# Attention: 4 of a unit's 16 transfers of turned weights issued by ScalarE, the other 12 by SyncE

## The chip, the cores and the metric

The kernel runs on one NeuronCore of a Trainium2 chip. The core has a matrix engine (TensorE, PE in the profile; its weight loads are shown apart as PEld), a vector engine (VectorE, DVE), an activation engine (ScalarE, ACT), a general engine (GpSimd, POOL) and an engine that mostly issues DMA transfers (SyncE, SP). Each engine works through its own list of instructions in order; semaphores tie the lists together. Data moves between HBM and the on-chip memory (SBUF, 128 partitions), and from one place of SBUF to another, by 16 DMA engines, which transfers issued by SyncE and ScalarE reach by a queue each. Matmuls write into PSUM, eight banks of 128 x 512 floats.

The metric is device time in microseconds, as the median of several runs. The profiler records one further execution instruction by instruction.

## The reference

The model is a "macaron" block in float32: half a feed-forward block, causal attention, half a feed-forward block again, on 16 sequences of 512 tokens of width 256. Only the attention bears on the change:

```python
x = x + 0.5 * ffn(layernorm(x))
x = x + attn(layernorm(x))          # the change is in here
x = x + 0.5 * ffn(layernorm(x))

def attn(x, Wq, bq, Wkv, bkv, Wo, bo):            # 16 heads, 64 wide
    q = x @ Wq + bq
    k, v = split(x @ Wkv + bkv)
    q, k = rope(q), rope(k)
    scores = einsum('bhqd,bhkd->bhqk', q, k) / sqrt(64)
    scores = where(causal, scores, -inf)
    probs = softmax(scores)
    out = einsum('bhqk,bhkd->bhqd', probs, v)
    return out.reshape(b, s, 1024) @ Wo + bo
```

## The kernel before

The program has three stages: the first feed-forward block, attention (from about 450 to 1930 us of the span) and the second feed-forward block. The change touches attention alone.

Attention is cut into 64 units: 16 sequences times four groups of four heads. A unit's weights, that is its softmax probabilities, are four tiles of 128 query rows (tile i has (i+1) x 128 keys, the causal part) for each of four heads. The loop over u near the end of `attention` is a pipeline written out by hand: in one turn of it the kernel makes queries and keys of unit u+3, scores and probabilities of unit u+2, turns the probabilities of unit u+1, and multiplies the turned ones of unit u by v and by the output weights. The order of the calls in that loop is the order of each engine's list; no scheduler moves them.

The steps by name and line:

- `scores` (L1047, L1054, TensorE) writes the products of queries and keys into PSUM banks p_as, tile 3 first, then 2, and in a later place tiles 1 and 0.
- `exps` (L1073, L1077): for each head and tile VectorE adds the mask, takes the row's extreme (amn) and moves the scores from PSUM to SBUF (pr), which empties the bank; ScalarE then makes the exponentials and their row sums (ars).
- `scaled` (L1082, L1085): VectorE inverts the sums, GpSimd multiplies pr by them.
- `turn`, `turn_most`, `turn_corner`, `turn_tile` (L1100, VectorE): the probabilities must stand with the keys on the partitions before they can be multiplied by v. VectorE can transpose squares of 32 x 32 within a group of 32 partitions; it writes the turned squares into the tile sq.
- `move` (L1127, SyncE): the squares of sq still have to change groups of partitions. 16 transfers do that: for each group k of 32 partitions of the result prT and each group q of sq, 32 rows of 5,120 bytes, 160 KB. All 16 move 2.6 MB, from SBUF to SBUF. They are issued when the last turn of the unit, `turn_tile(0)`, is done.
- `sums` (L1158, TensorE, p_av) multiplies prT by v; ScalarE copies the result to aoT (L1169).
- `leave` (L1176, TensorE, p_ay; L1182, VectorE): multiplies aoT by the output weights and adds to x; after a sequence's last group SyncE stores x (L1184).
- `values` (L1010 TensorE, L1013 ScalarE) makes v of the next unit.
- `Trip` (L961 VectorE, L964 and L970 SyncE) turns the normalized input of a coming sequence by way of HBM: one transfer out (away) and sixteen back (ahT), eight in each of two units, every fourth unit.

sq and prT have one buffer each, shared by all units. So the first turn of the next unit, `turn_most(0)`, can begin only when all 16 transfers have read sq, and the first transfer only when `sums` of the unit before has read prT. SyncE issues in one list, in this order: the 16 transfers of a unit, then, in some units, the write of away, two stores of x and eight reads of ahT.

The lines of the loop around the change:

```python
                if new:
                    new.scores((3,))
                    new.scores((2,))
                    new.exps((3,), slice(0, 1))
                if old and 0 <= u < nu - 2:
                    old.turn_tile(0)
                    old.move()
                if new:
                    new.exps((3,), slice(1, 2))
```

The transfers go out between the first and the second head's exponentials of tile 3 on ScalarE's side; ScalarE has its exponentials of heads 1 to 3 of tile 3 and of all heads of tile 2 still to do then.

Of the kernel before, what the change touches and what calls it, by code (L numbers as in the profile page):

```python
# [9 lines left out]
F32 = mybir.dt.float32  # L10
# [5 lines left out]
P = 128  # L16
# [18 lines left out]
HG = 4  # L35
NHG = AH // HG
SQ = 32
NSQ = P // SQ
# [9 lines left out]
def macaron_kernel(ctx: ExitStack, tc: tile.TileContext, a: dict, out: bass.AP):  # L48
    nc = tc.nc
# [835 lines left out]
    def attention(qp, wq, wk, wv, wo, cos, sin, row):  # L885


        ap = None
# [22 lines left out]
        nu = len(units)  # L911
        hTs, hs, qs, ks, vs, oTs, prTs, stds, trips = {}, {}, {}, {}, {}, {}, {}, {}, {}
# [11 lines left out]
        def scales(g, std):  # L924

            n = PB * NT
            rstds[g] = small.tile([P, n], F32, tag=f"rstd{g}", name=f"rstd{g}", bufs=1)
            nc.vector.reciprocal(rstds[g], std)
            pair_shift(g)

        def enter(b):

            hs[b] = [qp.tile([P, 2, D], F32, tag=f"rope{2 + k}", name=f"h{b}_{k}") for k in range(2)]
            for t in range(NT):
                i = (b % PB) * NT + t
                nc.scalar.activation(hs[b][t // 2][:, t % 2, :], xs[b][:, t, :], AF.Identity,
                                     bias=shifts[b // PB][:, i:i + 1], scale=rstds[b // PB][:, i:i + 1])
# [5 lines left out]
        def width(b):  # L943
            hTs[b] = qp.tile([P, NC, S], F32, tag="hT", name=f"ahT{b}", bufs=2)
            for c in range(NC):
                pt = ps(f"p_ahT{b}_{c}")
                for t in range(NT):
                    nc.tensor.transpose(pt[:, t * P:(t + 1) * P], hs[b][t // 2][:, t % 2, c * P:(c + 1) * P], ident)
                nc.scalar.copy(hTs[b][:, c, :], pt)  # L949
# [52 lines left out]
        def values(u, t0):  # L1002
            b, hg = units[u]
            if t0 == 0:
                pool, tag, bufs = (ap, "v", 1) if u + 1 < nu else (qp, "hT", 2)
                vs[u] = pool.tile([P, NT, HG * DQ], F32, tag=tag, name=f"v{b}_{hg}", bufs=bufs)
            pv = ps(f"p_v{b}_{hg}_{t0}")
            for t in range(2):
                for k in range(NC):
                    nc.tensor.matmul(pv[:, t * 256:(t + 1) * 256], hTs[b][:, k, (t0 + t) * P:(t0 + t + 1) * P],  # L1010
                                     wv[:, k, hg * HG * DQ:(hg + 1) * HG * DQ],
                                     start=(k == 0), stop=(k == NC - 1))
            nc.scalar.copy(vs[u][:, t0:t0 + 2, :].rearrange("p t d -> p (t d)"), pv)  # L1013
# [4 lines left out]
        blocks = NT * (NT + 1) // 2  # L1018
# [3 lines left out]
        class Weights:  # L1022
# [96 lines left out]
            def move(self):  # L1119

                prT = prTs[self.u] = ap.tile([P, NSQ, HG, blocks * SQ], F32, tag="prT", name=f"prT{self.nm}")
                for n in range(NSQ):
                    for k in range(NSQ):
                        q = (k + n) % NSQ
                        nc.sync.dma_start(prT[k * SQ:(k + 1) * SQ, q, :, :], self.sq[q * SQ:(q + 1) * SQ, k, :, :])  # L1127

            def turn_at_once(self, tag, vector):

# [59 lines left out]
        def queries_keys(u):  # L1190

            if u >= nu:
                return []
            q = qs[u] = Rotated(u, "q", wq, R_BQ)
            k = ks[u] = Rotated(u, "k", wk, R_BK)
            return [lambda: q.half(0), lambda: (q.half(1), q.add()), lambda: k.half(0), lambda: (k.half(1), k.add())]
# [4 lines left out]
        ap = yield [lambda: width(0)] + queries_keys(0)  # L1201
        ws = {}
        seen = 2 * NHG
        with tc.tile_pool(name="awayh", bufs=2, space=bass.MemoryType.DRAM) as away, \
                tc.manual_schedule(engines={mybir.EngineType.DVE, mybir.EngineType.Activation,
                                            mybir.EngineType.Pool, mybir.EngineType.SP}):
            for u in range(-2, nu):
                new = ws[u + 2] = Weights(u + 2) if u + 2 < nu else None
                qk = queries_keys(u + 3)
                old = ws.get(u + 1)  # L1210

                fresh = units[u + 5][0] if NHG < u + 5 < nu and units[u + 5][1] == 0 else 1 if u + 3 == NHG else None

                stats = [divmod(at, NHG) for at in range(seen, min(u + 15, NB * NHG))]
                seen = max(seen, u + 15)
                left = [divmod(u - NHG - 1, NHG)] if u >= NHG + 1 else []
                if u + 2 == nu:
                    old.scaled((1, 0))
                    values(u + 1, 0)
                    values(u + 1, 2)  # L1220
                if u >= 0:
                    sums(u, 0)
                    sums(u, 1)
                if fresh:
                    enter(fresh)
                if u + 4 in trips:
                    trips[u + 4].land((0, 1))
                if u + 3 in trips:
                    trips[u + 3].land((2, 3))
                if old and u + 2 == nu:  # L1230
                    old.turn_at_once("sq", range(0, 10, 2))
                elif u == -1:
                    values(0, 0)
                    values(0, 2)
                    old.turn_at_once("prT", range(2, 10, 3))
                elif old:
                    old.scaled((1, 0), slice(0, HG // 2))
                    old.turn_most(1)
                    old.turn_most(2)
                    old.scaled((1, 0), slice(HG // 2, HG))  # L1240
                    old.turn_most(3)
                    old.turn_corner()
                    old.turn_tile(1)
# [9 lines that stand above are left out]
                gone = [leave(u, 0)] if u >= 0 else []  # L1253
                if fresh == 1:
                    width(1)
                if u >= 0:
                    gone.append(leave(u, 2))
                if new:
                    new.exps((3,), slice(2, HG))
                    new.exps((2,), halfway=lambda: new.scaled((3,)))  # L1260
                if u == -2:
                    new.scaled((2,))
                    new.scores((1, 0))
                    new.exps((1, 0))
                    new.scaled((1, 0))
                if u + 6 in stds:
                    scales((u + 6) // (PB * NHG), stds.pop(u + 6))
                if fresh and fresh > 1:
                    trips[u + 5] = Trip(fresh)

                if u == nu - NHG + 1:
                    for g in range(NB // PB - 1):
                        pair_rstd(g)
                if u == nu - 1:
                    for g in range(PB):
                        entered[g] = xs[g]
                        for t in range(NT):
                            i = (g % PB) * NT + t
                            nc.vector.tensor_scalar(xs[g][:, t, :], xs[g][:, t, :], mvs[g // PB][:, i, 0:1],
                                                    rstds[g // PB][:, i:i + 1], ALU.subtract, ALU.mult)  # L1280
                for one in gone:
                    one()
                if new and u > -2:
                    new.scaled((2,))
                for one in stats + left:
                    token_stats(*one)
                for one in qk:
                    one()
                if fresh:
                    with_bias(fresh)  # L1290
                if NHG < u + 7 < nu and (u + 7) % (PB * NHG) == 0:
                    stds[u + 7] = spread((u + 7) // (PB * NHG))
                if 0 <= u < nu - 2:
                    values(u + 1, 0)
                    values(u + 1, 2)
                if new and u > -2:
                    new.scores((1, 0))
                    if u + 3 < nu:
                        new.turn_most(0)
                    new.exps((1, 0))  # L1300
            token_stats(NB - 2, NT - 1)
# [55 lines left out]
```

## Time and profile before

| what | us |
|---|---|
| runs | 2311.49, 2314.21, 2315.38 |
| median of the runs | 2314.21 |
| the profiled execution, its time | 2317.09 |
| its span, first to last instruction | 2315.4 |
| attention, 460 to 1890 us of the span: TensorE busy | 1417.9 of 1430 |
| the same: VectorE, ScalarE, GpSimd busy | 1269.4, 780.2, 845.1 |
| the same: mean share of the 16 DMA engines | 0.55 |
| granted TensorE clock, mean | 0.995 of full speed |
| transfers prT<-sq | 992 (62 units x 16), 160 KB each |

How to read it: a row of the profile names the line, the engine, the operation and the tiles, output before input. Behind the bar stand the busy time and the mean duration of one, then the idle time of the engine before such instructions and what ended it. "SPq" and "ACTq" are DMA issues, which occupy an engine's list but are not counted as busy time. A timeline row gives start, duration, engine, line, operation and, in brackets, the idle time before it with its releaser. Matmuls overlap in the hardware, so a busy TensorE row says that it was not starved, not that it ran at its peak.

Two of the 64 units turn their probabilities on TensorE (`turn_at_once`), so 62 have transfers.

### The profile page before, as it was taken

How to read it: one execution, taken by the hardware profiler on the slowest of the kernel's cores; microseconds unless marked ns; L12 is line 12 of the kernel's file. 1: busy time of each engine (PE TensorE's matmuls, PEld its weight loads, DVE VectorE, ACT ScalarE, POOL GpSimd, SP SyncE). 2: the span in 40 equal slices, each digit the busy share in tenths (PEclk: the TensorE clock that was granted, in tenths of full speed). 3: DMA queues.
4: the chain of work that ended last, by engine and by line, in shares of the span. 5: the costliest groups of instructions: out<-in, count | busy, mean ns of one | idle time of the engine just before them, and what ended most of it. 6: DMA issues, size and time to landing. Idle time of an engine off the chain costs nothing. (4 is left out here: it accounts for less than half of the span.)

```text
span 2315.4 us, 52884 instructions
## 1 busy us (share of the span) xinstructions
PE 2254.7 (97%) x19544; PEld 1488.2 (64%) x19544; DVE 1761.6 (76%) x4678; ACT 1158.1 (50%) x3296; POOL 1068.6 (46%) x1695
## 2 busy tenths in 40 slices
PE   7999999999999999999999999999999999998999
PEld 4764488566666666666666666666666666764588
DVE  5742298788889898989898988989888875432387
ACT  5753243455555555556464545555555555532233
POOL 2210054565566556565656565656556542210043
PEclk9999999999999999999999999999999999999999
DMA  6839851055556465554655554646455543739734
GB/s 209 261 112 403 339 140 55 7 131 121 130 127 147 110 148 130 122 140 111 146 129 129 128 140 111 158 97 160 120 132 130 124 115 112 237 138 404 305 116 140
DMA packets 221929, 359.52 MB, mean 155 GB/s; under 512 B 99876, under 2 KB 159848, under 8 KB 213480
## 3 DMA queue, kind: packets, MB, share of 16 engines
q1 hardware_dynamic: 220812, 355.34, 55.3%
q8 instruction: 155, 2.54, 0.5%
q14 instruction: 102, 0.84, 0.1%
q10 hardware_dynamic: 860, 0.81, 0.1%
HBM read 156.29 MB, written 37.22 MB: 84 GB/s over the span
## 5 line engine op out<-in xcount | busy, mean ns | idle before, releaser
L1085 POOL TENSOR_SCALAR pr<-pr,ars 128x512 f32<-128x512 f32 (+3 forms) x1024 | 524.1, 532 | 575.0 <-DVE ars L1082 573.8
L1077 ACT ACTIVATE pr<-pr,amn 128x512 f32<-128x512 f32 (+3 forms) x1024 | 561.8, 550 | 219.6 <-DVE amn L1073 215.2
L1100 DVE STREAM_TRANSPOSE sq<-pr 128x768 f32<-128x768 f32 x434 | 384.5, 918 | 130.1 <-DMA prT<-sq 106.7
L1073 DVE CUSTOM_DVE_ANT_0 pr<-p_as,causal 128x512 f32<-128x512 f32 (+2 forms) x768 | 308.6, 457 | 7.0 <-PE p_as L1054 5.8
L1054 PE MATMUL p_as<-k,q 32*64 32x448 f32 (+3 forms) x8192 | 307.3, 414 | 0.0
L1158 PE MATMUL p_av<-prT,v 128*64 128x512 f32 (+3 forms) x2048 | 291.5, 437 | 10.1 <-ACT pr L1077 2.0
L1013 ACT COPY v<-p_v 128x512 f32<-128x512 f32 x128 | 74.6, 585 | 451.3 <-PE p_v L1010 451.3
L1158 PEld LDWEIGHTS p_av<-prT,v 128*64 128x64 f32 x2048 | 161.1, 137 | 139.6 <-issue 92.7
L1176 PE MATMUL p_ay<-wo,aoT 128*128 128x256 f32 x1024 | 238.6, 386 | 4.1 <-DVE amn L1073 3.0
L1010 PE MATMUL p_v<-wv,ahT 128*128 128x256 f32 x1024 | 231.6, 379 | 0.7 <-DVE x L1182 0.7
L988 PE MATMUL p_q<-ahT,wq 128*128 128x512 f32 x512 | 230.6, 593 | 0.2 <-ACT ahT L949 0.2
L1054 PEld LDWEIGHTS p_as<-k,q 32*64 32x64 f32 x8192 | 201.8, 131 | 45.0 <-issue 26.2
L988 PE MATMUL p_k<-ahT,wk 128*128 128x512 f32 x512 | 230.3, 592 | 0.0
L1176 PEld LDWEIGHTS p_ay<-wo,aoT 128*128 128x128 f32 x1024 | 189.2, 190 | 62.2 <-DVE amn L1073 37.0
L1010 PEld LDWEIGHTS p_v<-wv,ahT 128*128 128x128 f32 x1024 | 194.5, 190 | 53.8 <-issue 23.7
L1077 ACT ACTIVATION_READ_ACCUMULATOR pr<-pr,amn 128x1 f32 x1024 | 192.0, 187 | 0.0
L988 PEld LDWEIGHTS p_k<-ahT,wk 128*128 128x128 f32 x512 | 97.3, 190 | 122.0 <-issue 106.9
L988 PEld LDWEIGHTS p_q<-ahT,wq 128*128 128x128 f32 x512 | 97.0, 190 | 95.7 <-issue 78.6
L1073 DVE CUSTOM_DVE_ANT_1 pr<-p_as,causal 128x384 f32<-128x384 f32 x256 | 130.2, 546 | 0.0
L1169 ACT ACTIVATE aoT<-p_av,bcol 128x128 f32<-128x128 f32 (+1 forms) x384 | 117.1, 391 | 9.9 <-PE p_av L1158 9.9
L584 PE MATMUL p_ds<-hT,qk 128*128 128x512 f32 x256 | 118.8, 609 | 2.1 <-ACT hT L159 2.1
L811 PE MATMUL p_cy<-vw,catT 128*128 128x256 f32 x512 | 120.8, 379 | 0.0
(179 smaller groups left out, 3358.0 us busy)
## 6 DMA issues: line engine op xcount, KB each, us to landing
prT<-sq SPq DMA_DIRECT2D x992, 160.0 KB
w<-in_e_W_dram SPq DMA_DIRECT2D x64, 1024.0 KB
w<-in_e_Wg_dram SPq DMA_DIRECT2D x32, 1024.0 KB
out_dram<-x SPq DMA_DIRECT2D x64, 256.0 KB
awaya<-sqa SPq DMA_DIRECT2D x25, 512.0 KB
atT<-awaya SPq DMA_DIRECT2D x100, 128.0 KB
xl<-in_attn_x_dram SPq DMA_DIRECT2D x16, 512.0 KB
xl<-out_dram SPq DMA_DIRECT2D x16, 512.0 KB
```

The lines of the kernel that those rows point to most:

```text
L584: nc.tensor.matmul(psc, qk[:, k, c * P:(c + 1) * P], hT[:, k, :], start=(k == 0), stop=(k == NC - 1))
L811: nc.tensor.matmul(py[:, t * D:(t + 1) * D], atT[:, c, t * P:(t + 1) * P], vws[b][:, c, :], start=(c == 0), stop=(c == NC - 1))
L988: nc.tensor.matmul(pq, self.w[:, k, at:at + P], hTs[self.b][:, k, :], start=(k == 0), stop=(k == NC - 1))
L1010: nc.tensor.matmul(pv[:, t * 256:(t + 1) * 256], hTs[b][:, k, (t0 + t) * P:(t0 + t + 1) * P], wv[:, k, hg * HG * DQ:(hg + 1) * HG * DQ], s ...
L1054: nc.tensor.matmul(banks[j][half * H:(half + 1) * H, at:at + wh], q[n][rows, q0:q0 + H], k[n][rows, :wh], start=(n == 0), stop=(n == 1))
L1073: nc.vector.tensor_tensor_reduce(out=by_block(self.at(i, j)), in0=by_block(banks[j][:, at:at + w]), in1=mask(i), scale=-1.0 / math.sqrt(DQ ...
L1077: nc.scalar.activation(self.at(i, j), self.at(i, j), AF.Exp, bias=self.mn[:, i, j:j + 1], scale=-1.0, accum_out=self.rs[:, i, j:j + 1])
L1085: nc.gpsimd.tensor_scalar(self.at(i, j), self.at(i, j), self.rs[:, i, j:j + 1], 1.0, ALU.mult, ALU.mult)
L1100: nc.vector.transpose(view(self.sq, j * blocks * SQ + dst[0] * SQ, [(blocks * SQ, nh)] + [(s * SQ, n) for s, (_, n) in zip(dst[1:], of)] + ...
L1158: nc.tensor.matmul(po[j * DQ:(j + 1) * DQ, :].rearrange("d (a f) -> d a f", a=NSQ)[:, :, t * SQ:], vs[u][:, t, head * DQ:(head + 1) * DQ], ...
L1169: nc.scalar.activation(dst[:, odd, to], src[:, odd, of], AF.Identity, bias=bcol[:, r:r + 1])
L1176: nc.tensor.matmul(py[:, t * D:(t + 1) * D], oTs[u][:, pair, (t0 + t) * P:(t0 + t + 1) * P], wo[:, hg * (HG // 2) + pair, :], start=(pair ...
```

## The change

`move` now issues twelve of the sixteen transfers on SyncE: those of the first three rounds n. The four of the last round (n = 3) become a function of their own, `move_rest`, in another order of k, and go to ScalarE's queue. `move_rest` is called after the exponentials of tile 2, so ScalarE issues them when it has done those. What each transfer copies is as before.

```diff
-                prT = prTs[self.u] = ap.tile([P, NSQ, HG, blocks * SQ], F32, tag="prT", name=f"prT{self.nm}")
-                for n in range(NSQ):
-                    for k in range(NSQ):
-                        q = (k + n) % NSQ
-                        nc.sync.dma_start(prT[k * SQ:(k + 1) * SQ, q, :, :], self.sq[q * SQ:(q + 1) * SQ, k, :, :])
+                prTs[self.u] = ap.tile([P, NSQ, HG, blocks * SQ], F32, tag="prT", name=f"prT{self.nm}")
+                self.send(nc.sync, [(k, (k + n) % NSQ) for n in range(NSQ - 1) for k in range(NSQ)])
+
+            def move_rest(self):
+
+                self.send(nc.scalar, [(k, (k + NSQ - 1) % NSQ) for k in (2, 3, 0, 1)])
+
+            def send(self, queue, ways):
+                for k, q in ways:
+                    queue.dma_start(prTs[self.u][k * SQ:(k + 1) * SQ, q, :, :],
+                                    self.sq[q * SQ:(q + 1) * SQ, k, :, :])
...
                 if new:
                     new.exps((3,), slice(2, HG))
                     new.exps((2,), halfway=lambda: new.scaled((3,)))
+                if old and 0 <= u < nu - 2:
+                    old.move_rest()
                 if u == -2:
```

## Prediction

> **What bounds the kernel now.** I read the busy shares and costliest groups of the page first, then the attention stage (460 to 1890 us, where all the moved transfers are issued) in the table by windows, then one unit engine by engine in the timelines.
>
> ```profile
> PE 2254.7 (97%) x19544; PEld 1488.2 (64%) x19544; DVE 1761.6 (76%) x4678; ACT 1158.1 (50%) x3296; POOL 1068.6 (46%) x1695
> ...
> L1100 DVE STREAM_TRANSPOSE sq<-pr 128x768 f32<-128x768 f32 x434 | 384.5, 918 | 130.1 <-DMA prT<-sq 106.7
> ...
> L1176 PEld LDWEIGHTS p_ay<-wo,aoT 128*128 128x128 f32 x1024 | 189.2, 190 | 62.2 <-DVE amn L1073 37.0
> ```
>
> TensorE is nearly always busy, but two waits show beside it: VectorE waits 106.7 us for the transfers prT<-sq, and TensorE's weight loads for p_ay wait 37.0 us for VectorE. They are one loop. Here is a unit whose transfers begin at t0 = 1047.09, SyncE, VectorE and TensorE in turn:
>
> ```profile
> 1047.09 10.05 SPq L1127 DMA_DIRECT2D prT<-sq  x16
> ...
> 1060.97 0.98 DVE L1100 STREAM_TRANSPOSE sq<-pr 128x768 f32<-128x768 f32 x1 [2.10 <-DMA prT<-sq]
> 1062.04 0.42 DVE L1073 CUSTOM_DVE_ANT_0 pr<-p_as,causal 128x256 f32<-128x256 f32 x1
> ...
> 1060.43 0.22 PE L1047 MATMUL p_as<-blank 32*64 32x64 bf16 x4
> ...
> 1069.72 1.99 PE L1176 MATMUL p_ay<-wo,aoT 128*128 128x256 f32 x8
> ```
>
> The 16 transfers are issued in 10.05 us; the turn of head 0 (turn_most(0), which overwrites sq) can start only when all have landed, at t0+13.88. After it come the row maxima of tiles 1 and 0, and 7.68 us after the first of them (1062.04) p_ay starts, as soon as VectorE has emptied a bank of tile 3 (1069.00 + 0.65). So the loop is: landing, turn, maxima, turns, bank, p_ay, next t0.
>
> I listed these starts for all 61 units from the timelines. Between successive p_ay the 60 intervals sum to 1405.3 us; the usual one is 23.26, so 9.7 us in all lie above it. Usually the maxima start 1.61 us after TensorE's p_as for tiles 1 and 0 (1060.43 to 1062.04): the matmuls set the pace, and a landing some 0.17 us later would cost nothing (the turn needs about 0.9 us before the maxima, so it may start up to t0+14.04; the median of the 33 units of 60 that meet this is t0+13.88). The other 27 of 60 turns start later. In the 25 later than t0+14.1 the interval grows nearly one for one, 8.8 us in all. One such unit, t0 = 578.66:
>
> ```profile
> 593.23 0.98 DVE L1100 STREAM_TRANSPOSE sq<-pr 128x768 f32<-128x768 f32 x1 [2.78 <-DMA prT<-sq]
> ...
> 601.78 1.56 PE L1176 MATMUL p_ay<-wo,aoT 128*128 128x256 f32 x6 [0.21 <-DVE amn L1073]
> ```
>
> The turn starts at t0+14.57, p_ay at t0+23.12 instead of t0+22.63. What counts is therefore one number, the landing of the last of 16. Shifting all 61 turn starts and summing what lies above 14.04 gives the price: earlier by 0.2 us -4.7 us, by 0.5 us -8.7, never more than -9.8; later by 0.13 us +4.6, by 0.2 us +7.6, by 0.4 us +18.8. There is no more to gain than 9.8 us, as TensorE's own work sets 23.26.
>
> What sets the landing is seen in the table by windows of the first unit (time, PE, PEld, DVE, ACT, POOL, clock, share of the 16 DMA engines, GB/s):
>
> ```profile
> 1047.10:1048.20 1.10, 1.10 (x7) 0.97 (x6) 1.10 (x5) 0.76 (x3) 0.00 (x0) 1.00 0.00 0
> 1048.20:1050.00 1.80, 1.80 (x10) 1.59 (x9) 1.69 (x9) 1.80 (x7) 0.00 (x0) 1.00 0.94 205
> 1050.00:1052.00 2.00, 2.00 (x6) 0.95 (x5) 2.00 (x7) 2.00 (x7) 1.81 (x3) 1.00 0.95 276
> 1052.00:1054.00 2.00, 2.00 (x6) 0.88 (x5) 1.85 (x7) 1.95 (x5) 2.00 (x5) 1.00 0.97 223
> 1054.00:1056.00 2.00, 2.00 (x6) 0.83 (x5) 2.00 (x4) 1.39 (x2) 1.54 (x3) 1.00 1.02 225
> 1056.00:1058.00 2.00, 2.00 (x9) 1.37 (x8) 2.00 (x4) 0.00 (x0) 2.00 (x2) 1.00 1.05 228
> 1058.00:1060.00 2.00, 2.00 (x11) 1.77 (x10) 0.87 (x2) 0.58 (x1) 1.88 (x3) 1.00 0.82 177
> 1060.00:1061.00 1.00, 1.00 (x31) 0.67 (x37) 0.03 (x1) 0.46 (x1) 0.69 (x1) 1.00 0.02 5
> ```
>
> Nothing moves for 1.1 us after the first issue; then the DMA engines are full, at about 223 GB/s, until just before 1060. 16 transfers of 163,840 bytes at 223 GB/s are 11.8 us, 0.735 each, while SyncE issues one each 10.05/16 = 0.63 us. The engines, not the issuing queue, are the limit, and a queue of about a microsecond of work stands before them from the middle on. 1.1 + 11.8 leaves 1.0 of the 13.88 us for the start-up and for the last completion to reach VectorE.
>
> **The change, part by part.** Call SyncE's transfers S0 to S11 and ScalarE's A0 to A3.
>
> *Taken off SyncE*: four issues of 0.63 us, 2.5 us a unit. Since the engines are full, the issues shorten nothing by themselves: 0.
>
> *Put on ScalarE*: four issues behind its exponentials of tile 2. Its six issues at the start of the kernel took 0.24 to 0.59 us, so 1.0 to 2.4 us a unit, plus 239 more semaphore instructions in the build, about four a unit, at 17 to 28 ns (SyncE's shortest and median at L1127): 0.1. The exponentials end at t0+5.18 in nearly every unit and ScalarE's next work, the copy of v, follows 6.59 us after (1005.4 to 1012.00 in the unit of t0 = 1000.23). In every eighth unit two table loads, a square root and an exponential (3.1 us) stand between, and 3.4 us of idle time remain. Hidden: 0. Without that cover the copy of v would be late, then av behind it on TensorE, 1.0 to 2.5 us a unit.
>
> *The wait that is added*, not seen in the diff. The build gives DMAs eight completion semaphores in turn, and each DMA waits until the one before it on its semaphore has landed. In 61 of 62 units the turns are taken in the order S0 S1 S2 S3 A0 S4 A1 S5 A2 S6 A3 S7 S8 S9 S10 S11. So S8 waits for A0's landing and S10 for A1's; A2 and A3 wait for S0 and S2, long landed. S8 is no longer issued at t0+5.0: A0 goes out at about t0+5.3, its data can move from t0+6.4, and S7 is still in the engines until 1.1 + 0.4 + 8 x 0.735 = t0+7.4 (0.4 us for the start-up). A0, sharing them with S6 and S7, is done by t0+8.1 and landed by about t0+8.6; S8 follows 3.6 us later than now, with data from t0+9.7. By then the engines have A1 to A3 to do, until 1.5 + 12 x 0.735 = t0+10.3. So they do not run dry, by 0.6 us. S9 to S11 come 0.63 us apart and are served 0.735 apart; the sixteenth ends at 1.5 + 11.8 = t0+13.3 and lands at t0+13.9, as now: 0. Bounds: earlier by 0.5 us if the queues together move more than one (-8.7), later by 0.3 us if the engines run dry for that long (+12.9). I take 0, because the share of 0.94 to 1.05 leaves no room in the one direction and the 0.6 us is room in the other.
>
> *Behind S11 on SyncE* stand the write of turned x (L964), two stores of y (L1184) and eight reads back (L970), now about a microsecond later (S11's issue ends at t0+11.2, not 10.05). In the unit of t0 = 1000.23 the reads began at 1016.06, took 4.85 us, and the next transfers of turned weights went out at 1023.83: 2.9 us free, so 0; with it gone, the next t0 is late one for one.
>
> *Order elsewhere*: VectorE's and GpSimd's instructions and waits are the same in both builds; TensorE's are too, but for a wait or two.
>
> *The late units.* 20 of the 992 issues on SyncE took 0.92 to 1.70 us instead of 0.59, mostly 96 instructions apart, and 16 KB instruction transfers of 0.9 to 1.3 us lie among them; one DMA engine then ends later than the others. SyncE has 248 instructions fewer (1804 instead of 2052), ScalarE 487 more: two to three such fetches fewer here, five more there, each worth 8.8/25 = 0.35 us when it meets the transfers, about half the time on ScalarE. Sum 0, bounds -1 and +2.
>
> **A rule and the rows.** A1 writes partitions 96 to 127 while S8 writes 0 to 31, so they might use different paths. No transfer from two queues at once is in this trace; the windows stay at 223 to 228 GB/s although neighbours on one queue already write different halves. The Trainium skill, "DMA: Bandwidth & Descriptors", Rules for kernel authors, speaks against the change: two transfers to disjoint partition halves serialize, since both use the same 16 engines, from one queue or two. The skill's "SBUF — State Buffer", "Can I just issue two DMAs to hit both halves?", gives 6% for such a pair; on the four transfers that would be an estimated 0.18 us a unit, some -4 us by my price list, where the rows say 0.
>
> **Sum.** 0 against the profiled execution: span 2315.4 us, its time 2317.1 with 1.7 us around it. The median of the runs, 2314.2, lies 2.9 us below that, so I forecast 2314 us.
>
> **Rivals.** *Faster*: two queues keep the DMA engines better filled; the last landing comes 0.5 us earlier, the late units vanish, 2314.2 - 8.7 = 2305.5 us. For it: 27 late turns are there to be saved, and A0 to A3 are out before S8. Against: the full share; A0 and A1 write the same half as S6 and S7, A3 the same as S8.
> *Slower*: the wait of S8. If A0 lands after about t0+9.2, S8 brings its data after the engines have run dry, and each further tenth delays the last landing by a tenth. With A0 at t0+9.6 the landing is 0.4 us late: 2314.2 + 18.8 = 2333 us; 0.2 us gives 2322. For it: A0 depends on ScalarE's issue, nowhere measured beside work, and passes through a queue that SyncE's backlog shares. Against: it needs 0.6 us more than the rows give.
> *ScalarE held up*: its four issues outlast 6.59 us; it would take 1.6 us each against at most 0.59 seen. Under 2 in 100, counted as slower.
>
> **How the numbers follow.** No change 0.46, faster 0.27, slower 0.27. About 0.2%, 4.6 us, is what a measurement can tell from no change; by the price list that is a landing between 0.2 us earlier and 0.13 us later, a narrow gate for a forecast of this kind, which is why no change does not get more. Its own range is 2310 to 2318; for 8 in 10 it reaches over the faster case to 2305 and into the slower one to 2326.
>
> **What would show it.** Right: SyncE's transfers split 8 and 4, with a gap of about 3.5 us waiting for ScalarE's; VectorE's wait for prT<-sq still near 2 us; p_ay intervals of 23.26. Wrong on the faster side: more than 240 GB/s over 2 us while both queues are at work, and turn starts before t0+13.5. Wrong on the slower side: a DMA share clearly below 0.9 near t0+9 to t0+11, turns after t0+14.1 in most units and more than 37 us of weight loads waiting for VectorE.

## The result and the profile after

The changed kernel takes 2324.0 us (median of 5 runs, 2322.2 to 2328.0); the kernel before, beside it, 2314.2 (2311.5 to 2316.0). The ratio is 1.0043, 95% interval 1.0028 to 1.0058: slower by 9.8 us, where no change was forecast. The profiled execution took 2327.98 us, with a span of 2326.3.

From the page of the changed kernel, busy times of the engines, the first two DMA queues (packets, MB, share of the 16 engines' span) and two of the costliest groups:

```profile
PE 2259.2 (97%) x19544; PEld 1482.4 (64%) x19544; DVE 1759.7 (76%) x4678; ACT 1158.7 (50%) x3296; POOL 1072.3 (46%) x1695
...
q1 hardware_dynamic: 208908, 314.69, 47.7%
q10 hardware_dynamic: 12764, 41.45, 8.0%
...
L1100 DVE STREAM_TRANSPOSE sq<-pr 128x768 f32<-128x768 f32 x434 | 385.1, 918 | 148.6 <-DMA prT<-sq 102.5
...
L1182 PEld LDWEIGHTS p_ay<-wo,aoT 128*128 128x128 f32 x1024 | 189.1, 190 | 69.9 <-DVE amn L1073 45.8
```

ScalarE's queue (q10) now carries its quarter. VectorE idles 148.6 us before its turns instead of 130.1; the row names the releaser of most of it, the transfers prT<-sq, whose own figure even falls (106.7 to 102.5); the view of waits puts 37.9 us instead of 23.4 down to ahT<-away. TensorE's weight loads for p_ay wait 45.8 us for VectorE instead of 37.0. So the same loop is longer. The 60 intervals between successive p_ay sum to 1418.5 us instead of 1405.3 (+13.2). With t0 as the moment at which a unit's first transfer goes out, the start of turn_most(0) has its median at t0+14.41 instead of t0+14.01, and 47 of 60 turns start after t0+14.1 instead of 26. Here is the unit of t0 = 1170.09, which has this median, in the timelines of SyncE, ScalarE, VectorE and TensorE:

```profile
1170.09 4.31 SPq L1132 DMA_DIRECT2D prT<-sq  x7
...
1175.13 0.51 SPq L1132 DMA_DIRECT2D prT<-sq  x1
...
1178.13 2.74 SPq L1132 DMA_DIRECT2D prT<-sq  x4
...
1174.34 0.52 ACTq L1132 DMA_DIRECT2D prT<-sq  x1
1174.48 0.19 ACT L1077 ACTIVATION_READ_ACCUMULATOR pr<-pr,amn 128x1 f32 x1
1174.58 0.60 ACT L1077 ACTIVATE pr<-pr,amn 128x384 f32<-128x384 f32 x1
1174.89 0.61 ACTq L1132 DMA_DIRECT2D prT<-sq  x1
1175.08 0.19 ACT L1077 ACTIVATION_READ_ACCUMULATOR pr<-pr,amn 128x1 f32 x1
1175.54 1.33 ACTq L1132 DMA_DIRECT2D prT<-sq  x2
...
1184.51 0.98 DVE L1100 STREAM_TRANSPOSE sq<-pr 128x768 f32<-128x768 f32 x1 [2.64 <-DMA prT<-sq]
...
1193.07 2.21 PE L1182 MATMUL p_ay<-wo,aoT 128*128 128x256 f32 x9 [0.22 <-DVE amn L1073]
```

Three things are to be seen. SyncE's list has gaps: S0 to S6 go out as before, S7 at t0+5.04, S8 only at t0+8.04. A0 goes out at t0+4.25, while ScalarE still has its last exponential of tile 2 to do (1174.58 to 1175.18): the issues run ahead of the engine's own work. So it is not right that ScalarE issues them when it has done the exponentials, as the section on the change says. And the turn starts at t0+14.42, so that p_ay waits.

The landings of the single transfers, taken from the semaphore events in the trace (medians over 60 units), say where S7 and S8 stood: S3 lands at t0+5.05 and S7 goes out at 5.07; A0 lands at 8.05 and S8 goes out at 8.06; A1 lands at 9.21 and S10 goes out at 9.46 (within a unit 0.02 to 0.7 us behind A1, 0.1 in the median). The last of the 16 lands at t0+14.12 instead of t0+13.84.

### The profile page after: what moved, and what is told of

Same layout as the page of the kernel before. It is cut to its first block, busy times and chain, and to the rows that moved or that the text cites. A ratio compares the mean times of both kernels' runs of the same rounds, so it can differ in the third digit from the quotient of the medians.

```text
span 2326.3 us, 53123 instructions
## 1 busy us (share of the span) xinstructions
PE 2259.2 (97%) x19544; PEld 1482.4 (64%) x19544; DVE 1759.7 (76%) x4678; ACT 1158.7 (50%) x3296; POOL 1072.3 (46%) x1695
## 5 line engine op out<-in xcount | busy, mean ns | idle before, releaser
L1100 DVE STREAM_TRANSPOSE sq<-pr 128x768 f32<-128x768 f32 x434 | 385.1, 918 | 148.6 <-DMA prT<-sq 102.5
L1013 ACT COPY v<-p_v 128x512 f32<-128x512 f32 x128 | 74.8, 586 | 437.5 <-PE p_v L1010 430.9
L1182 PEld LDWEIGHTS p_ay<-wo,aoT 128*128 128x128 f32 x1024 | 189.1, 190 | 69.9 <-DVE amn L1073 45.8
L1054 PEld LDWEIGHTS p_as<-k,q 32*64 32x64 f32 x8192 | 193.5, 131 | 48.2 <-issue 30.6
```

The lines of the kernel that those rows point to most:

```text
L1054: nc.tensor.matmul(banks[j][half * H:(half + 1) * H, at:at + wh], q[n][rows, q0:q0 + H], k[n][rows, :wh], start=(n == 0), stop=(n == 1))
L1100: nc.vector.transpose(view(self.sq, j * blocks * SQ + dst[0] * SQ, [(blocks * SQ, nh)] + [(s * SQ, n) for s, (_, n) in zip(dst[1:], of)] + ...
L1182: nc.tensor.matmul(py[:, t * D:(t + 1) * D], oTs[u][:, pair, (t0 + t) * P:(t0 + t + 1) * P], wo[:, hg * (HG // 2) + pair, :], start=(pair ...
```

## The experiments

A transfer writes 32 partitions of prT (group k) and reads 32 partitions of sq (group q). Groups 0 and 1 lie in the lower half of the partitions (L), 2 and 3 in the upper (U). The packets of 5,120 bytes take 351 ns on average instead of 341. In the later part of a unit of the kernel before, they take 380 to 400 ns where neighbouring transfers write one half, and the time dips to 310 to 330 where the half changes. Read transfer by transfer in the order of issue, the written halves are LLUU LLUU LLUU LLUU before, and LLUU LLUU UULL LLUU in the change: ScalarE's order k = 2, 3, 0, 1 puts S6, S7, A0 and A1 into U, and A2, A3, S8 and S9 into L. So there are three theories. **A**, order of halves: a transfer is slower behind one of the same half, and the change puts four in a row. **B**, waits: S7, S8 and S10 go out late and the DMA engines run short. **C**, two queues: serving two queues costs by itself.

The first four runs set them against each other. The last landing is in each case the median over the units, counted from t0.

**e1, the split kept, ScalarE's order 0, 1, 2, 3** (written halves as before, in the order of the code):

```diff
-                self.send(nc.scalar, [(k, (k + NSQ - 1) % NSQ) for k in (2, 3, 0, 1)])
+                self.send(nc.scalar, [(k, (k + NSQ - 1) % NSQ) for k in range(NSQ)])
```

> The changed kernel, with ScalarE's four transfers in the order k = 0, 1, 2, 3 instead of 2, 3, 0, 1, so that behind S6 and S7, which write partitions 64 to 127, come two that write 0 to 63. Queues, waits and counts as in the changed kernel. Theory A (order of halves: a transfer is slower behind one that writes the same half of the partitions, and the change puts four of a half in a row): most of the 10 us goes, 2313 to 2319 us, turns of head 0 at a median of t0+14.1 or earlier. Theory B (waits: S7 waits for S3, S8 for A0, S10 for A1, and the DMA engines run short) and theory C (serving two queues costs the DMA engines time by itself): 2324 us within 3.

Measured: 2314.99 us, ratio 1.0003 (0.9994 to 1.0012), last landing t0+13.86. The loss is gone, with two queues and with the gaps still there (S8 goes out at t0+7.89). The turns start at a median of t0+14.14, a little behind the 14.1 that theory A named, and the 60 intervals sum to 1407.9 us, so a rest of 2 or 3 us can't be excluded.

**e2, all 16 on SyncE, in the order of the change** (against the kernel before):

```diff
-                for n in range(NSQ):
-                    for k in range(NSQ):
-                        q = (k + n) % NSQ
-                        nc.sync.dma_start(prT[k * SQ:(k + 1) * SQ, q, :, :], self.sq[q * SQ:(q + 1) * SQ, k, :, :])
+                ways = [(k, (k + n) % NSQ) for n, ks in ((0, (0, 1, 2, 3)), (1, (0, 1, 2, 3)), (3, (2, 3, 0, 1)), (2, (0, 1, 2, 3))) for k in ks]
+                for k, q in ways:
+                    nc.sync.dma_start(prT[k * SQ:(k + 1) * SQ, q, :, :], self.sq[q * SQ:(q + 1) * SQ, k, :, :])
```

> The kernel before, all 16 transfers on SyncE, in the order in which the changed kernel has them: rounds 0 and 1, then ScalarE's four (k = 2, 3, 0, 1 of round 3), then round 2. One queue and no new waits. Theory A: slower than before by 4 to 12 us, 2318 to 2326 us, turns at a median of t0+14.2 or later. Theories B and C: 2314 us within 3, turns at t0+14.0.

Measured: 2324.1 us, ratio 1.0043 (1.0031 to 1.0056), last landing t0+14.12, packets 351 ns. The whole loss, with one queue and without a gap.

**e3, all 16 on SyncE, k = 0, 2, 1, 3 in every round** (the half changes at every step):

```diff
+                ways = [(k, (k + n) % NSQ) for n in range(NSQ) for k in (0, 2, 1, 3)]
```

> The kernel before, all 16 transfers on SyncE, k in the order 0, 2, 1, 3 in every round, so that each transfer writes the other half than the one before it. Theory A: the last lands 0.4 us earlier or more; with the price list of the prediction 2305 to 2309 us, and p_ay intervals of 23.26 nearly throughout. Theories B and C: no change, 2314 us within 3.

Measured: 2301.64 us, ratio 0.9946 (0.9933 to 0.9958), last landing t0+12.83, packets 302 ns. Faster than both kernels, and than the 2305 to 2309 expected.

**e4, the split, both queues in an alternating order**:

```diff
-                self.send(nc.sync, [(k, (k + n) % NSQ) for n in range(NSQ - 1) for k in range(NSQ)])
+                self.send(nc.sync, [(k, (k + n) % NSQ) for n in range(NSQ - 1) for k in (0, 2, 1, 3)])
...
-                self.send(nc.scalar, [(k, (k + NSQ - 1) % NSQ) for k in (2, 3, 0, 1)])
+                self.send(nc.scalar, [(k, (k + NSQ - 1) % NSQ) for k in (2, 0, 3, 1)])
```

> The changed kernel with alternating halves in both queues: SyncE k = 0, 2, 1, 3 in rounds 0 to 2, ScalarE k = 2, 0, 3, 1. Waits and queues as in the changed kernel. Theory A: 2305 to 2316 us, well under the changed kernel. Theories B and C: 2324 us within 3.

Measured: 2304.31 us, ratio 0.9959 (0.9945 to 0.9972), last landing t0+13.10. The order brings most of it with the split too; the split adds nothing.

The four agree with A alone: B and C would have left e1 slow and e2 as before. The tables by windows show the same. First the kernel before, its unit of t0 = 1164.42, in steps of 2.5 us from t0+2.5 (time, PE, PEld, DVE, ACT, POOL, clock, share of the 16 DMA engines, GB/s):

```profile
1166.92:1169.42 2.50, 2.50 (x8) 1.32 (x7) 2.39 (x9) 2.50 (x10) 1.91 (x3) 1.00 0.86 254
1169.42:1171.92 2.50, 2.50 (x7) 1.14 (x6) 2.34 (x8) 0.18 (x2) 2.50 (x6) 1.00 0.98 221
1171.92:1174.42 2.50, 2.50 (x7) 1.14 (x6) 2.50 (x5) 0.00 (x0) 2.04 (x3) 1.00 1.06 229
1174.42:1176.92 2.50, 2.50 (x13) 2.21 (x12) 1.78 (x3) 0.58 (x1) 2.38 (x3) 1.00 1.01 223
```

The same unit of e2, in the order of the change:

```profile
1170.08:1172.58 2.50, 2.50 (x8) 1.32 (x7) 2.38 (x9) 2.50 (x10) 1.92 (x3) 1.00 0.87 246
1172.58:1175.08 2.50, 2.50 (x7) 1.14 (x6) 2.34 (x8) 0.18 (x2) 2.50 (x6) 1.00 1.02 225
1175.08:1177.58 2.50, 2.50 (x8) 1.14 (x6) 2.50 (x5) 0.00 (x0) 2.03 (x3) 1.00 1.03 215
1177.58:1180.08 2.50, 2.50 (x13) 2.22 (x12) 1.77 (x3) 0.59 (x1) 2.37 (x3) 1.00 1.03 215
```

And of e3:

```profile
1158.34:1160.84 2.50, 2.50 (x8) 1.31 (x7) 2.38 (x9) 2.50 (x10) 1.92 (x3) 1.00 0.90 256
1160.84:1163.34 2.50, 2.50 (x7) 1.14 (x6) 2.34 (x8) 0.18 (x2) 2.50 (x6) 1.00 0.92 244
1163.34:1165.84 2.50, 2.50 (x8) 1.14 (x7) 2.50 (x5) 0.00 (x0) 2.03 (x3) 1.00 0.91 250
```

From the second row on the share is about full in the first two and lower in e3, but what the engines move differs: 221 to 229 GB/s before, 215 where four of a half follow each other, 244 to 250 where the halves alternate. A share of 1.00 says that the engines hold packets, not how fast these go. In e3 the issues, 0.635 us apart, are nearly the limit again, but not yet: its transfers land 0.68 us apart, and the time from issue to landing still grows, from 2.62 us for the first to 3.27 for the last.

The next four ask which half decides, the written or the read one. In e3 the read halves alternate nearly as often as the written ones, 13 changes of 15. e5 and e6 part the two, e7 has runs of a length between (its reads, too, come in runs of up to four), e8 asks whether it is the half or the group of 32 partitions. Each replaces the list `ways` of e2, as pairs (k, q):

```diff
+                ways = ((0, 0), (2, 1), (1, 0), (3, 1), (0, 1), (2, 0), (1, 1), (3, 0), (0, 2), (2, 3), (1, 2), (3, 3), (0, 3), (2, 2), (1, 3), (3, 2))   # e5
+                ways = ((0, 0), (1, 2), (0, 1), (1, 3), (1, 0), (0, 2), (1, 1), (0, 3), (2, 0), (3, 2), (2, 1), (3, 3), (3, 0), (2, 2), (3, 1), (2, 3))   # e6
+                ways = ((0, 0), (1, 1), (0, 1), (1, 2), (2, 2), (3, 3), (2, 3), (3, 0), (0, 2), (1, 3), (0, 3), (1, 0), (2, 0), (3, 1), (2, 1), (3, 2))   # e7
+                ways = ((0, 0), (0, 1), (2, 2), (2, 3), (1, 1), (1, 2), (3, 3), (3, 0), (0, 2), (0, 3), (2, 0), (2, 1), (1, 3), (1, 0), (3, 1), (3, 2))   # e8
```

**e5, writes alternate, reads in runs of eight.**

> All 16 transfers on SyncE; the halves of partitions that they write alternate (15 changes of half), the halves that they read come in two runs of eight (1 change). Theory A as 'the written half counts': like the alternating order of the batch before, last landing about t0+12.8, packets about 302 ns, 2302 us. Rival 'the read half counts': the reads are then at their worst, the last landing later than before (after t0+14.1), slower than 2324 us. If both count about equally: near 2314 us.

Measured: 2344.4 us, ratio 1.0129 (1.0104 to 1.0154), last landing t0+14.42.

**e6, reads alternate, writes in runs of eight.**

> All 16 on SyncE; the written halves come in two runs of eight (1 change of half), the read halves alternate (15 changes). 'The written half counts': one change of half was worth 0.13 us so far (7 changes landed at t0+13.84, 15 at t0+12.83; 5 at t0+14.11), so with 1 change the landing is at t0+14.6 to 14.7, 0.8 us later, some +45 us: about 2355 us; packets 370 ns or more. 'The read half counts': 2302 us.

Measured: 2349.79 us, ratio 1.015 (1.0121 to 1.018), last landing t0+14.54, packets 372 ns.

The written half alone does not decide, and neither does the read half: a run of eight on either side is slow, though the other side alternates. "About equally, near 2314" fell as well. In e5's unit of t0 = 1176.82, by windows:

```profile
1179.32:1181.82 2.50, 2.50 (x8) 1.32 (x7) 2.38 (x9) 2.50 (x10) 1.91 (x3) 1.00 0.98 205
1181.82:1184.32 2.50, 2.50 (x7) 1.14 (x6) 2.34 (x8) 0.18 (x2) 2.50 (x6) 1.00 0.99 197
1184.32:1186.82 2.50, 2.50 (x7) 1.14 (x6) 2.50 (x5) 0.00 (x0) 2.04 (x3) 1.00 0.92 240
1186.82:1189.32 2.50, 2.50 (x13) 2.21 (x12) 1.77 (x3) 0.58 (x1) 2.37 (x3) 1.00 0.98 201
```

About 200 GB/s while eight transfers read L, 240 in the window in which the reads go over to U, 201 again after it. The landings say the same: within the runs of e5 they come 0.81 us apart (163,840 bytes in 0.81 us are 202 GB/s). At the change of half the last of the run comes 1.01 behind the one ahead and the next three 0.73, 0.65 and 0.57, on average 0.74.

**e7, writes in runs of four.**

> All 16 on SyncE, written halves in four runs of four: 3 changes of half. If each change of the written half is worth 0.13 us: last landing t0+14.4, 0.5 us later than before, some +25 us by the price list of the prediction continued: about 2338 us. If only a first repetition costs and longer runs cost no more: near the 2324 us of the change.

Measured: 2339.24 us, ratio 1.0106 (1.008 to 1.0131), last landing t0+14.36: near the 2338 of a price for each change, far from the 2324 of a first repetition alone. As its reads run to four as well, it does not say which side costs.

**e8, one group of 32 partitions twice, then the other half.**

> All 16 on SyncE; each transfer is followed by one that writes the very same 32 partitions, then the half changes: 7 changes of half as in the kernel before, but the pairs write one quarter instead of two quarters of a half. If what counts is the half: as before, last landing t0+13.8 to 13.9, 2310 to 2318 us. If it is the quarter of 32 partitions (or the same rows): a different time, slower by more than 5 us.

Measured: 2312.59 us, ratio 0.9994 (0.9982 to 1.0005), last landing t0+13.72. What counts is the half: twice the same group is no worse than two groups of a half.

Two counting rules fitted the kernel before, the change and these one-queue runs: steps at which both halves change (before 5, change 3, e3 13, e5 to e7 1 each, e8 5), or the number of changes on the side that has fewer (7, 5, 13, 1, 1, 3, 7). e9 and e10 have orders for which the rules differ. e11 and e12 ask whether the split costs anything once the order is right; e11 differs from e4, the others from the kernel before.

```diff
+                ways = ((0, 0), (2, 1), (3, 2), (0, 3), (1, 0), (3, 1), (2, 2), (1, 3), (0, 1), (2, 0), (3, 3), (0, 2), (1, 1), (3, 0), (2, 3), (1, 2))   # e9
+                ways = ((0, 0), (1, 1), (2, 2), (3, 3), (0, 1), (1, 0), (2, 3), (3, 2), (0, 3), (1, 2), (2, 0), (3, 1), (0, 2), (1, 3), (2, 1), (3, 0))   # e10
-                self.send(nc.scalar, [(k, (k + NSQ - 1) % NSQ) for k in (2, 0, 3, 1)])   # e4
+                self.send(nc.scalar, [(k, (k + NSQ - 1) % NSQ) for k in (2, 0, 1, 3)])   # e11
+                ways = ((0, 0), (2, 2), (0, 1), (2, 3), (1, 0), (3, 2), (1, 1), (3, 3), (0, 2), (2, 0), (0, 3), (2, 1), (1, 2), (3, 0), (1, 3), (3, 1))   # e12
```

**e9, at each step one half changes, never both.**

> All 16 on SyncE. From one transfer to the next either the written half changes or the read half, never both and never neither: 8 changes of the written half, 7 of the read half, 0 steps at which both change. Theory 'a step helps only where both halves change' (both: kernel before 5, the change 3, e3 13, e5, e6 and e7 1 each): with 0 such steps last landing t0+14.4 to 14.6 or later, 2340 to 2355 us. Rival 'the side with fewer changes decides' (7 here, 7 in the kernel before): last landing t0+13.8, about 2313 us.

Measured: 2305.6 us, ratio 0.9972 (0.996 to 0.9984), last landing t0+13.56.

**e10, both halves change together, in pairs.**

> All 16 on SyncE. The halves change together: 7 changes of the written half, 6 of the read half, 6 steps at which both change and 8 at which neither does. Theory 'a step helps only where both change': 6 against 5 of the kernel before, at 0.13 us each: last landing t0+13.7, 2308 to 2312 us. Rival 'the side with fewer changes decides' (6): between the kernel before (7) and the change (5): landing t0+13.95 to 14.0, about 2318 us.

Measured: 2312.25 us, ratio 0.9999 (0.9991 to 1.0008), last landing t0+13.85.

Both rules fell: e9 is far from the 2340 of the first and better than the 2313 of the second, and e10 lands where the kernel before does (13.84), neither at 13.7 nor at 13.95 and later; its time, at the upper edge of the first rule's, does not decide. What holds over all orders is the length of the runs on the worse side, in steps and not as a formula:

| runs of one half on the worse side | kernels | last landing, t0+ | time against before |
|---|---|---|---|
| one, a few of two | e3, e12 | 12.83, 12.90 | 0.995 |
| two (e1, as its transfers land: one of three among the writes, three of three among the reads; e10: one of four among the reads) | before, e1, e8, e9, e10 | 13.56 to 13.86 | 0.997 to 1.000 |
| two of four, the others two | the change, e2 | 14.12 | 1.004 |
| four | e7 | 14.36 | 1.011 |
| eight | e5, e6 | 14.42, 14.54 | 1.013, 1.015 |

**e11, the split with halves alternating as they reach the engines.**

> The change's split of 12 and 4, with SyncE's rounds in the alternating order and ScalarE's four in such an order that the halves alternate as the transfers of the two queues reach the DMA engines (written halves of S6, A0, A1, S7, A2, A3, S8: 0 1 0 1 0 1 0). If the split itself costs nothing, e4's 2.7 us over the one alternating queue came from repeats of a half: the same as e3, 2300 to 2302.5 us, last landing t0+12.9 or sooner. If the waits of S7, S8 and S10 cost something when the engines are not full: 2303 to 2306 us, landing at t0+13.1 as in e4.

Measured: 2304.73 us, ratio 0.9963 (0.9949 to 0.9976), last landing t0+13.15.

**e12, one queue, both sides alternating.**

> All 16 on SyncE, 14 of 15 steps change both halves (e3: 13). The issues of 0.635 us each already set the landing in e3, so the same time is expected by every theory: 2299 to 2304 us, last landing t0+12.8; it serves as the measure for the split beside it.

Measured: 2301.69 us, ratio 0.9947 (0.9934 to 0.9959), last landing t0+12.90. Its transfers land 0.69 us apart, so here too the issues alone, 0.635 us apart, do not set the landing.

The two splits stand at 2304.3 and 2304.7, the two with one queue at 2301.6 and 2301.7. The intervals overlap, but the profiles point the same way: the last landings are 0.2 to 0.3 us later with the split, and the 60 intervals sum to 1398.9 and 1400.4 us against 1397.3 and 1396.9.

But e11 did not get the order that it was made for, S6, A0, A1, S7. In its unit of t0 = 1158.43 S7 goes out at t0+4.75 and A1 at 4.78:

```profile
1163.18 0.51 SPq L1132 DMA_DIRECT2D prT<-sq  x1
...
1163.21 0.62 ACTq L1132 DMA_DIRECT2D prT<-sq  x1
```

S7 lands ahead of A1 in 49 of the 62 units, as in e4, so A0 and S7 follow each other in one half, and then A1 and A2. The tenth landing is already late, t0+9.12 against 8.84 in e12, and the sixteenth is no later than that (13.15 against 12.90): the 0.25 us arise around A0, S7 and A1, not behind the late S8 and S10. The view of waits has SyncE's transfers wait for earlier ones as follows (total, times, longest us), first in the changed kernel:

```profile
SPq L1132 <- DMA prT<-sq: 306.4, 219, 4.0
```

in e11:

```profile
SPq L1132 <- DMA prT<-sq: 269.1, 242, 4.4
```

and in e12:

```profile
SPq L1126 <- DMA prT<-sq: 79.2, 71, 2.8
```

With the order mended, the split makes SyncE wait 190 us more in all (269.1 - 79.2). In the order of the kernel before such waits were covered (287.3 us of them in e1, at a ratio of 1.0003). Whether the 2 to 3 us by which e4 and e11 stand behind e3 and e12 come from the wait of S7 or from the halves that still repeat, these runs do not settle.

## Why the prediction was wrong

*What bounds the kernel*: right. Where the last transfer landed late, its landing set turn, maxima, bank and p_ay; where it landed early (e3, e12), nearly all the intervals are 23.26, TensorE's own.

*The price list*: right. The last landing came 0.28 us later; between +7.6 for 0.2 us and +18.8 for 0.4 us that is +12. The intervals grew by 13.2 us in the profiled execution, the runs by 9.8 (6.5 to 13.4 by the interval of the ratio). To the other side, "never more than -9.8" held for the loop as well: e3 and e12 took 8.0 and 8.4 us out of the 60 intervals. Their runs gained 11.8 us. What lies ahead of the 60 intervals and behind them takes 898.6 (e12) to 910.1 us (the kernel before) in the profiled executions, 901.8 in e3, but 903.3 in e10 too, which gained nothing; so the rest can't be placed. (The turns later than t0+14.1 in the kernel before are 26, not 25; nothing hangs on it.)

*Issues taken off SyncE, 0, and ScalarE's own work, 0*: right. The exponentials still end at t0+5.18. But A0 was taken to go out "at about t0+5.3", behind them; it goes out at t0+4.25, ahead of the engine.

*The added wait*: the wait was right and its list incomplete. S8 waited for A0 as foretold, 3 us later than now instead of 3.6. Overlooked were S6 and S7, which through A2 and A3 came to wait for S1 and S3: S7 lost 0.7 us. That the engines "do not run dry" was nearly right. Their mean share falls to 0.94, 0.89 and 0.93 in the half microseconds from t0+9.5, near the "clearly below 0.9" that the prediction named as the mark of this wait. Taken for the mark, the dip would have led to the wrong cause: e1 has the same one (0.89, 0.87, 0.94) and no loss.

*The step that failed* is the end of that part: "served 0.735 apart; the sixteenth ends at 1.5 + 11.8 = t0+13.3 and lands at t0+13.9, as now: 0". It took 0.735 us for what a transfer costs, when it is what a transfer costs in the order of the kernel before, in pairs of a half. In e2 the third transfer of each run of four lands 0.82 us after the one ahead, and the whole run costs about 0.14 us more than two pairs, half of the 0.28 us that the two runs of the change make. The bound "later by 0.3 us (+12.9)" held the size, for another reason.

*The evidence was there.* The prediction wrote that "A0 and A1 write the same half as S6 and S7, A3 the same as S8", and used it only against a gain. And "the windows stay at 223 to 228 GB/s although neighbours on one queue already write different halves" read pairs as if they were alternation: every second neighbour wrote the same half. The packets of the trace before already told the two kinds of neighbour apart, 380 to 400 ns and 310 to 330.

*The rule weighed against the rows.* The Trainium skill, "DMA: Bandwidth & Descriptors", Rules for kernel authors, has two transfers to disjoint halves serialize, and "SBUF — State Buffer", "Can I just issue two DMAs to hit both halves?", allows such a pair 6%. Here the same 16 engines take 0.81 us a transfer in a run on one half and 0.68 where halves alternate on one queue, 16% less, which is a rate higher by 19%. So the measurement decides for more than 6%. As to two queues as such, the rule of the first of these pages holds: e1 stands at 1.0003.

*The rivals.* Faster: two queues in the old order of halves brought no earlier landing (e1: t0+13.86 against 13.84). Slower, by S8's wait: 2322 for 0.2 us was of the right size by luck, as the wait is there in e1 without the loss. ScalarE held up: not seen; it still stands idle for 430.9 us in all before the copies of v (451.3 before).

Open are why the half matters, and the exact rule: e9 (2305.6 us) beats the kernel before and e10 with runs no shorter. That the loss comes from the order of the halves, and not from the split, is shown by e1 and e2. What the 2 to 3 us are by which the splits stay behind once the halves alternate is open.

## What to carry to other kernels

When a change reorders transfers, the order is part of the change: write down, for each, the half of the partitions that it reads and the half that it writes, in the sequence in which they go out and land in the trace, before pricing anything else. With two queues that sequence is not the one written in the code, as e11 shows. A rate read from a window holds for the order in that window, and a DMA share of 1.00 does not say that the engines move what they can. Here a single list in an order of alternating halves (e3) was worth 11.8 us, and a second queue nothing.

## What the hardware showed beyond this

- Transfers of 32 partitions from SBUF to SBUF go at about 202 GB/s in a run on one half, whether the run is on the reading side (e5, landings 0.81 us apart) or on the writing side (e6, about 0.8 as well), at about 223 in pairs, and at 244 to 250 where the halves alternate.
- ScalarE's DMA issues run ahead of its own engine: A0 goes out 0.93 us before the last exponential ahead of it in the list ends, with its row sum.
- Queues of two engines are tied by the completion semaphores that they share: SyncE's S8 waits for ScalarE's A0, which neither the code nor the data asks for: it goes out 0.02 us after A0 has landed, 3 us later than before.
